# One head of each of four row groups per attention step, instead of two heads of each of two

## The chip, the core and the metric

The kernel runs on one core of a Trainium2 chip. The time is the device time of one launch in microseconds (us). Three runs of the kernel before gave 972.80, 970.39 and 972.62 us, median 972.62. All data is float32.

## The reference, cut to what matters

The reference is a two-layer transformer block on x of 4 sequences x 256 tokens x 512 features. Each layer is an attention and a feed-forward product, each followed by a residual sum and a layer norm. The change is in the attention of layer 0:

```python
q = (x @ Wq + bq).reshape(B, S, 32, 16)      # 32 query heads of 16
k = (x @ Wk + bk).reshape(B, S, 8, 16)       # 8 key heads, each serves 4 query heads
v = (x @ Wv + bv).reshape(B, S, 8, 16)
scores = q @ k.T / sqrt(16)                  # causal: a query sees the keys up to itself
p = softmax(where(causal, scores, -1e9))
out = (p @ v).reshape(B, S, 512) @ Wo + bo
```

Layer 1 has heads of 128 features and an ALiBi-like bias; the change doesn't touch it.

## The kernel before, in words

The program is written in a tile framework that draws the semaphores between the engines from what each instruction reads and writes, and that orders each engine's instructions when the program is built: it walks through the program with durations of its own, and lets an instruction that has to wait be passed by later ones. Each engine then runs its queue strictly in that order.

**Layer 0's attention.** `project0(b)` makes, for each of the four sequences b, `qT` and `kT` with the features on the partitions, and `v`. Partitions are read in four **row groups** of 32 rows. A row group r holds two key heads of 16 rows each, e = 0 and e = 1. `kT[:, e, :]` is the key tile with the rows of the other head set to zero, so that a product over the 32 rows of a group with `kT[rows, e]` gives the scores of head (r, e) alone. `qT[rows, i, :]` holds the i-th of the four query heads that share each key head.

A **step** is (b, qt, h, i): sequence, query tile of 128 queries (qt = 0 sees w = 128 keys, qt = 1 sees w = 256), pair of row groups h, query head i. There are 4 x 2 x 2 x 4 = 64 steps, and each works on four heads: row groups 2h and 2h+1, e = 0 and 1.

- `begin0` (lines 473 to 495): two score matmuls (L482), one for each row group, each 2w columns wide (both e), each into a PSUM bank of its own. So a step's tile `sc` takes two banks, and the pool `ps_s0` (L127) has two such tiles: four banks. Then VectorE adds the causal mask to the diagonal block (L487) and takes the negated row maxima (L490), and ScalarE makes four exponentials with row sums (L274, one for each head, each with an accumulator read after it). VectorE inverts the row sums (L279) and GpSimd multiplies the probabilities with them (L282), for the step before, through `divide0`.
- `transpose0` (L506 to L518), three steps later: TensorE transposes the four heads' probabilities, 128 x 128 at a time (L297), into a bank of the pool `ps_w`, and VectorE or ScalarE in turn (L100, L102) copies the bank to `prT`.
- `end0` (L520 to L541), after the fourth i of an h, with two steps more of delay: the value matmuls (L531). Each has 128 keys on the rows, 32 columns of `v` (one row group r, head e, the other head's 16 columns zero), and 512 moving columns (four i x 128 queries), and writes partitions 32r to 32r+31 of the bank `o`. The 32 columns are one **column group** of the array. Before the change the order is kt, e, then the two column groups of h. After h = 1 the bank is copied out and `tail0` (output product L438, layer norm, feed-forward product L455, layer norm) is queued.

Each float32 matmul of the program shows up in the trace as two matmul instructions, with two weight loads.

`run` (L323) issues the steps in the order begin, fill, transpose, end; `fill` advances the tails of the query tiles before (L438, L440, L455, L459, layer norms) and the projections of the sequence to come (L386, L399, L414). PSUM has 8 banks, all taken: 3 `ps_w`, 4 `ps_s0`, 1 `ps_o0`.

```python
    ps_s0 = pool(la, "ps_s0", 2, space=PSUM)
        sc = ps_s0.tile([P, 2, 2, 2 * P], F32, tag="s", name=f"sc_{name}")
        for j in range(2):
            rows = slice(32 * (2 * h + j), 32 * (2 * h + j) + 32)
```

Of the kernel before, what the change touches and what calls it, by code (L numbers as in the profile page):

```python
# [12 lines left out]
F32 = mybir.dt.float32  # L13
# [3 lines left out]
ALU = mybir.AluOpType  # L17
AX = mybir.AxisListType
PSUM = bass.MemoryType.PSUM

P = 128
B, S, D = 4, 256, 512
NTT = B * S // P
NC = D // P
NKV, G = 8, 4
BLK = 32
ROWS = 64
EPS = 1e-5
MASKED = -3.0e38

# [19 lines left out]
def distance_table():  # L52

    rel = P + np.arange(P)[:, None] - np.arange(2 * P)[None, :]
    dist = -np.sqrt(np.maximum(rel, 0).astype(np.float32))
    return np.where(rel >= 0, dist, np.float32(MASKED)).astype(np.float32)


@with_exitstack
def block_kernel(  # L60
# [20 lines left out]
    nc = tc.nc  # L81
    slopes = [float(s) for s in alibi_slopes()]

    def pool(stack, name, bufs=1, **kw):
        return stack.enter_context(tc.tile_pool(name=name, bufs=bufs, **kw))
# [9 lines left out]
    def evacuate(dst, src):  # L95

        if not last:
            turn[0] ^= 1
        if turn[0] and not last:
            nc.vector.tensor_copy(dst, src)  # L100
        else:
            nc.scalar.copy(dst, src)  # L102
# [18 lines left out]
    la = ctx.enter_context(ExitStack())  # L121
    wa = pool(la, "wa", side="right")
    a0 = pool(la, "a0", 2, side="right")
    causal = wa.tile([P, P], F32, name="causal")
    make_causal_mask(nc, causal, MASKED)
    ps_w = pool(ctx, "ps_w", 3, space=PSUM)
    ps_s0 = pool(la, "ps_s0", 2, space=PSUM)  # L127
    ps_o0 = pool(la, "ps_o0", 1, space=PSUM)
    ring = [ps_w, "w"]

# [102 lines left out]
    def load_weights1(kv):  # L233
        wq1 = w1.tile([P, NC, G * P], F32, tag="wq1", name=f"wq1_{kv}", bufs=1)
        wo1 = w1.tile([P, G, D], F32, tag="wo1", name=f"wo1_{kv}")
        if kv % 2 == 0:
            wk1 = w1.tile([P, NC, 2 * P], F32, tag="wk1", name=f"wk1_{kv}", bufs=1)
            nc.sync.dma_start(wk1, w_qkv_v[:, :, NQ + kv * P : NQ + (kv + 2) * P])
            wk_pair[kv // 2] = wk1
        nc.sync.dma_start(wq1, w_qkv_v[:, :, ts(kv, G * P)])  # L240
        weights1[kv] = (wq1, wo1)
        if kv == 0:
            load_output_weight(kv)
# [29 lines left out]
    def exponentials(pr, sc, nm, sums, i, w):  # L273
        nc.scalar.activation(  # L274
            pr[:, i, 0:w], sc, AF.Exp, bias=nm[:, i : i + 1], accum_out=sums[:, i : i + 1]
        )
# [9 lines left out]
    def softmax_tiles(sp, name, bufs):  # L286
        nm = sp.tile([P, G], F32, tag="nm", name=f"nm_{name}", bufs=bufs + 2)
        sums = sp.tile([P, G], F32, tag="sums", name=f"sums_{name}", bufs=bufs + 2)
        pr = sp.tile([P, G, 2 * P], F32, tag="pr", name=f"pr_{name}", bufs=bufs)
        return nm, sums, pr  # L290

    def transposed_probabilities(name, pr, parts):

        for kt, dst in parts:
            pt = bank_t(f"pt_{name}_{kt}")
            for i in range(G):
                nc.tensor.transpose(pt[:, i, :], pr[:, i, ts(kt, P)], ident)  # L297
            evacuate(dst, pt.rearrange("p i (j q) -> p i j q", q=32))
# [43 lines left out]
    def advance(queue):  # L342

        while queue:
            if next(queue[0], None) is not None:
                return
            queue.popleft()

    def exhaust(queue):
        while queue:  # L350
            advance(queue)
# [82 lines left out]
    def tail0(tt, oT):  # L434

        py = bank_m(f"py_{tt}")
        for i in range(G):
            nc.tensor.matmul(py, oT[:, i, :], wop[:, i, :], start=(i == 0), stop=(i == G - 1))  # L438
        y = s0.tile([P, D], F32, tag="y", name=f"y_{tt}")
        nc.vector.tensor_tensor(y, py, x[tt], ALU.add)  # L440
        factors = norm_factors(y, f"a{tt}")
        yield True
        x1 = s0.tile([P, D], F32, tag="x1", name=f"x1_{tt}")
        normalise(x1, y, factors)
        yield True
        if tt < NTT - 1:
            yield True
            yield True
        x1T = s0.tile([P, NC, P], F32, tag="x1T", name=f"x1T_{tt}")
        transposed(x1T, x1, f"x1_{tt}")  # L450
        nc.gpsimd.tensor_tensor(x1, x1, fb_b, ALU.add)
        yield True
        pf = bank_m(f"pf_{tt}")
        for c in range(NC):
            nc.tensor.matmul(  # L455
                pf, x1T[:, c, :], wfT[:, c, :], start=(c == 0), stop=(c == NC - 1)
            )
        y2 = s0.tile([P, D], F32, tag="y", name=f"y2_{tt}")
        nc.vector.tensor_tensor(y2, pf, x1, ALU.add)  # L459
        factors = norm_factors(y2, f"b{tt}")  # L460
        yield True
        x2[tt] = xp.tile([P, D], F32, tag="x", name=f"x2_{tt}")
        normalise(x2[tt], y2, factors)
        yield True
        if tt < NTT - 1:
            yield True
            yield True
        transposed(x2T[:, :, ts(tt, P)], x2[tt], f"x2_{tt}")
        yield True

    ahead, tails = deque(), deque()

    def begin0(b, qt, h, i):

        qT, kT, _ = qkv0[b]
        w = (qt + 1) * P
        name = f"0_{b}_{qt}_{h}_{i}"
        nm, sums, pr = softmax_tiles(a0, name, 6)
        sc = ps_s0.tile([P, 2, 2, 2 * P], F32, tag="s", name=f"sc_{name}")
        for j in range(2):  # L480
            rows = slice(32 * (2 * h + j), 32 * (2 * h + j) + 32)
            nc.tensor.matmul(  # L482
                sc[:, j, :, 0:w], qT[rows, i, ts(qt, P)], kT[rows, :, 0:w], start=True, stop=True
            )
        scf = sc.rearrange("p j e k -> p (j e) k")
        diag = scf[:, :, w - P : w]
        nc.vector.tensor_tensor(  # L487
            diag, diag, causal.unsqueeze(1).to_broadcast([P, G, P]), ALU.add
        )
        nc.vector.tensor_reduce(nm, scf[:, :, 0:w], AX.X, ALU.max, negate=True)  # L490
        for n in range(G):
            exponentials(pr, scf[:, n, 0:w], nm, sums, n, w)
        divide0()
        undivided.append((pr, sums, w))
        return pr

    open0 = {}
    undivided = []

    def divide0():  # L500


        if undivided:
            divided(*undivided.pop(), True)

    def transpose0(b, qt, h, i, pr):  # L506
        name = f"0_{b}_{qt}_{h}_{i}"
        if i == 0:
            open0["p", h] = a0.tile(
                [P, 2, G, 4, 4, 32], F32, tag="prT", name=f"prT0_{b}_{qt}_{h}"  # L510
            )
        prT = open0["p", h]
        transposed_probabilities(
            name,
            pr,
            [(kt, prT[:, kt, i].rearrange("p j n q -> p n j q")) for kt in range(qt + 1)],
        )
        return prT  # L518

    def end0(b, qt, h, i, prT):  # L520
        if i < G - 1:
            return
        if h == 0:
            open0["o"] = ps_o0.tile([P, G * P], F32, tag="o", name=f"o0_{b}_{qt}")
        o = open0["o"]
        v = qkv0[b][2]
        for kt in range(qt + 1):
            for e in range(2):
                for j in range(2):
                    r = 2 * h + j  # L530
                    nc.tensor.matmul(  # L531
                        o[32 * r : 32 * r + 32, :],
                        v[:, kt, r, ts(e, 32)],
                        prT[:, kt, :, :, 2 * j + e, :],
                        start=(kt == 0 and e == 0),
                        stop=(kt == qt and e == 1),
                    )
        if h == 1:
            oT = a0.tile([P, G, P], F32, tag="oT", name=f"oT0_{b}_{qt}")
            evacuate(oT.rearrange("p i q -> p (i q)"), o)  # L540
            tails.append(tail0(2 * b + qt, oT))  # L541

    def before0(step):
        b, qt, h, i = step
        if (qt, h, i) == (0, 0, 0):
            if b == 0:
                for _ in range(3):
                    advance(ahead)
            else:
                exhaust(ahead)  # L550
            if b + 1 < B:
                ahead.append(project0(b + 1))
            if b == 1:
                load_weights1(0)

    def fill():
# [3 lines left out]
    ahead.append(project0(0))  # L560
    tails.append(feed_forward_weight())
    run(
        [(b, qt, h, i) for b in range(B) for qt in range(2) for h in range(2) for i in range(G)],
        begin0,
        transpose0,
        end0,
        before0,
        fill,
        lag=3,
# [533 lines left out]
```

## Time and profile before

| what | value |
|---|---|
| median of three runs | 972.62 us (970.39 to 972.80) |
| the profiled execution's own time | 970.91 us |
| its span, first to last instruction | 968.9 us |
| mean granted TensorE clock | 0.995 |
| first to last score matmul of layer 0 (L482) | 14.1 to 253.7 us |
| first product of layer 1 (L632) | about 280 us |
| TensorE matmul busy, whole span | 97% |
| VectorE, ScalarE, GpSimd busy, whole span | 64%, 33%, 46% |

How to read it: times are us from the first instruction, single durations in ns. PE is TensorE's matmul, PEld its weight load, DVE VectorE, ACT ScalarE, POOL GpSimd. A "form" such as 32*128 32x512 is rows*columns of the array and the moving operand. The ends of matmuls are modelled, so that distances between starts are the better price of a matmul. Views of the trace used here: busy time by stretch, groups of instructions by line and form, the timeline, the chain of work, and waits.

### The profile page before, as it was taken

To read this page: it belongs to the slowest core of one execution; us is meant where nothing else is said; L and a number is where in the kernel's file an instruction comes from. 1 tells how busy PE (TensorE), PEld (TensorE's weight loads), DVE (VectorE), ACT (ScalarE), POOL (GpSimd) and SP (SyncE) were. 2 spreads that over 40 slices of the span, in tenths; PEclk is the share of its full clock that TensorE was granted. 3 is DMA by queue.
4 is the path that set the end of the run, shared out by engine and by line. 5 is a ranking of instruction groups with operands and counts; after the bars stand their busy time and mean duration, and the time that the engine had idled before them with its cause. 6 is when DMAs were issued, how large, how long until landed. Compare 5 with 4: busy or idle time off the path is not lost.

```text
span 968.9 us, 11389 instructions
## 1 busy us (share of the span) xinstructions
PE 939.5 (97%) x3593; PEld 556.0 (57%) x3593; DVE 619.7 (64%) x1291; ACT 316.3 (33%) x1194; POOL 445.6 (46%) x461
## 2 busy tenths in 40 slices
PE   7999999999899999999999999999999999999996
PEld 5645555554344445566666666666666666666652
DVE  3876767777633446665666665766676666666566
ACT  2664564555511002333222222122222212224441
POOL 3463552644446213444533553444633634556732
PEclk9999999999999999999999999999999999999998
DMA  9500000000020011354443443433443334332001
GB/s 237 185 1 1 1 1 1 1 1 1 1 87 0 22 44 39 103 139 120 122 134 90 123 133 109 130 109 87 131 130 91 128 77 119 113 105 69 1 33 55
DMA packets 76418, 74.45 MB, mean 77 GB/s; under 512 B 5957, under 2 KB 52678, under 8 KB 76358
## 3 DMA queue, kind: packets, MB, share of 16 engines
q1 hardware_dynamic: 75014, 72.02, 26.1%
q10 hardware_dynamic: 1344, 1.70, 0.6%
q8 instruction: 29, 0.48, 0.2%
q14 instruction: 31, 0.25, 0.1%
HBM read 49.58 MB, written 24.12 MB: 76 GB/s over the span
## 4 chain that ended last, share of the span: by engine, by line
PE 82%; POOL 9%; DVE 5%; ACT 2%; DMA 1%; issue 1%; ACTq 0%; POOLq 0%; DVEq 0%
PE p_q L632 18%; PE po L881 14%; PE sc L968 7%; PE o L1008 7%; PE p_k L632 5%; PE p_v L632 5%; PE o L531 5%; PE sc L482 4%; PE pt L297 3%; PE pq L399 3%; PE py L438 3%; PE pf L455 3%; PE py L842 2%; POOL pr L282 2%; POOL x L903 2%; ACT pr L274 1%
## 5 line engine op out<-in xcount | busy, mean ns | idle before, releaser
L274 ACT ACTIVATE pr<-sc,nm 128x256 f32<-128x256 f32 (+1 forms) x512 | 209.4, 420 | 364.7 <-DVE nm L984 277.2
L282 POOL TENSOR_TENSOR pr<-pr,sums 128x512 f32<-128x512 f32 (+1 forms) x128 | 190.1, 1485 | 232.1 <-DVE sums L279 223.9
L976 DVE SCALAR_TENSOR_TENSOR sc<-table,sc 128x128 f32<-128x128 f32 (+1 forms) x256 | 86.0, 356 | 34.7 <-PE sc L968 32.4
L274 ACT ACTIVATION_READ_ACCUMULATOR pr<-sc,nm 128x1 f32 x512 | 103.5, 202 | 0.0
L968 PEld LDWEIGHTS sc<-kT,qT 128*128 128x128 f32 x512 | 82.3, 191 | 35.1 <-issue 29.7
L968 PE MATMUL sc<-kT,qT 128*128 128x256 f32 (+1 forms) x512 | 95.0, 327 | 0.0
L1008 PE MATMUL o<-prT,v 128*128 128x512 f32 x192 | 92.8, 592 | 0.0
L308 DVE STREAM_TRANSPOSE blocks<-pr 128x512 f32<-128x512 f32 x84 | 57.6, 698 | 45.2 <-POOL pr L282 45.2
L646 DVE TENSOR_TENSOR qT<-p_q,qT 128x512 f32<-128x512 f32 x96 | 64.6, 685 | 33.6 <-PE p_q L632 32.8
L984 DVE TENSOR_REDUCE nm<-sc 128x2 f32<-128x512 f32 (+1 forms) x128 | 69.9, 550 | 1.5
L297 PE MATMUL pt<-ident,pr 128*128 128x128 f32 x432 | 62.6, 278 | 6.0 <-POOL pr L282 5.3
L297 PEld LDWEIGHTS pt<-ident,pr 128*128 128x128 f32 x432 | 49.3, 142 | 32.5 <-issue 17.1
L490 DVE TENSOR_REDUCE nm<-sc 128x4 f32<-128x512 f32 (+1 forms) x64 | 61.0, 953 | 1.1
L482 PE MATMUL sc<-kT,qT 32*128 32x256 f32 (+1 forms) x256 | 59.9, 533 | 1.6 <-ACT pr L274 1.6
L487 DVE TENSOR_TENSOR sc<-sc,causal 128x512 f32<-128x512 f32 x64 | 44.3, 692 | 26.5 <-PE sc L482 26.2
L881 PE MATMUL po<-wo,so 128*128 128x256 f32 x224 | 58.0, 381 | 2.1 <-POOL so L612 2.1
L632 PE MATMUL p_q<-x2T,ws_q 128*128 128x512 f32 x128 | 59.8, 592 | 0.0
L102 ACT COPY o<-o 128x512 f32<-128x512 f32 x29 | 17.0, 586 | 124.9 <-PE o L1008 124.9
L632 PE MATMUL p_q<-xt,ws_q 128*128 128x512 f32 x128 | 57.7, 592 | 0.0
L881 PE MATMUL po<-wo,o 128*128 128x256 f32 x224 | 57.7, 380 | 0.0
L632 PE MATMUL p_q<-x2T,wq 128*128 128x512 f32 x128 | 57.6, 592 | 0.0
L881 PE MATMUL po<-to,so 128*128 128x256 f32 x224 | 53.3, 381 | 1.0 <-POOL so L615 1.0
(155 smaller groups left out, 1435.2 us busy)
## 6 DMA issues: line engine op xcount, KB each, us to landing
way<-blocks SPq DMA_DIRECT2D x112, 128.0 KB, 2.5
prT<-way SPq DMA_DIRECT2D x28, 512.0 KB, 3.7
wq<-in_L_attn_w_qkv_dram SPq DMA_DIRECT2D x8, 1024.0 KB, 5.3
wo<-in_L_attn_w_o_dram SPq DMA_DIRECT2D x8, 1024.0 KB, 5.4
way<-blocks SPq DMA_DIRECT2D x112, 64.0 KB, 1.8
prT<-way SPq DMA_DIRECT2D x28, 256.0 KB, 2.6
wk<-in_L_attn_w_qkv_dram SPq DMA_DIRECT2D x4, 512.0 KB, 3.7
wv<-in_L_attn_w_qkv_dram SPq DMA_DIRECT2D x2, 1024.0 KB, 6.3
```

What stands on the lines that cost most here:

```text
L274: nc.scalar.activation(pr[:, i, 0:w], sc, AF.Exp, bias=nm[:, i : i + 1], accum_out=sums[:, i : i + 1])
L282: nc.gpsimd.tensor_tensor(pr[:, :, 0:w], pr[:, :, 0:w], sums.unsqueeze(2).to_broadcast([P, G, w]), ALU.mult)
L297: nc.tensor.transpose(pt[:, i, :], pr[:, i, ts(kt, P)], ident)
L482: nc.tensor.matmul(sc[:, j, :, 0:w], qT[rows, i, ts(qt, P)], kT[rows, :, 0:w], start=True, stop=True)
L490: nc.vector.tensor_reduce(nm, scf[:, :, 0:w], AX.X, ALU.max, negate=True)
L632: nc.tensor.matmul(bank, fixed, moving, start=(c == 0), stop=(c == 1))
L646: add = lambda dst, a, b: nc.vector.tensor_tensor(dst, a, b, ALU.add)
L881: nc.tensor.matmul(bank[:, ts(n, HALF)], left[:, c, :], right[:, c, :], start=(c == 0), stop=(c == 1),)
L968: nc.tensor.matmul(sc[:, m, 0:w], qT[:, 2 * j + m, b * S + qt * P : b * S + (qt + 1) * P], kT[:, b * S : b * S + w], start=True, stop=True,)
L976: nc.vector.scalar_tensor_tensor(sc[:, m, 0:w], table[:, 2 * P - w :], slopes[kv * G + 2 * j + m], sc[:, m, 0:w], ALU.mult, ALU.add,)
L984: nc.vector.tensor_reduce(nm[:, 2 * j : 2 * j + 2], sc[:, :, 0:w], AX.X, ALU.max, negate=True)
L1008: nc.tensor.matmul(o, v1[:, 2 * b + kt, ts(kv, P)], prT[:, kt].rearrange("p j h q -> p h j q"), start=(kt == 0), stop=(kt == qt),)
```

## The change

A step becomes (b, qt, e, i): one of the two heads e of each of **four** row groups. Its four score matmuls have w columns each (before: two with 2w), one in each of the four score banks. The pool of two tiles becomes one tile of four banks for the whole of layer 0, `scores0[P, 4, 2, 256]`, made once; the index in the third place, 0 or 1, is half a bank and alternates from step to step (`half0`). Mask, maxima, exponentials, transposes and copies keep their number and shapes; their third index now counts row groups. The value matmuls of an e go over the four column groups in turn; the accumulation of all four opens at e = 0 and closes at e = 1, four steps later. The number of value matmuls is the same.

```diff
-    ps_s0 = pool(la, "ps_s0", 2, space=PSUM)
+    ps_s0 = pool(la, "ps_s0", 1, space=PSUM)
...
+    scores0 = ps_s0.tile([P, 4, 2, 2 * P], F32, name="scores0")
+    half0 = [0]
+
+    def begin0(b, qt, e, i):
...
-        sc = ps_s0.tile([P, 2, 2, 2 * P], F32, tag="s", name=f"sc_{name}")
-        for j in range(2):
-            rows = slice(32 * (2 * h + j), 32 * (2 * h + j) + 32)
+        half0[0] ^= 1
+        sc = scores0[:, :, half0[0], :]
+        for r in range(4):
+            rows = slice(32 * r, 32 * r + 32)
             nc.tensor.matmul(
-                sc[:, j, :, 0:w], qT[rows, i, ts(qt, P)], kT[rows, :, 0:w], start=True, stop=True
-            )
-        scf = sc.rearrange("p j e k -> p (j e) k")
-        diag = scf[:, :, w - P : w]
+                sc[:, r, 0:w], qT[rows, i, ts(qt, P)], kT[rows, e, 0:w], start=True, stop=True
+            )
+        diag = sc[:, :, w - P : w]
...
-            exponentials(pr, scf[:, n, 0:w], nm, sums, n, w)
+            exponentials(pr, sc[:, n, 0:w], nm, sums, n, w)
...
-    def end0(b, qt, h, i, prT):
+    def end0(b, qt, e, i, prT):
...
         for kt in range(qt + 1):
-            for e in range(2):
-                for j in range(2):
-                    r = 2 * h + j
-                    nc.tensor.matmul(
-                        o[32 * r : 32 * r + 32, :],
-                        v[:, kt, r, ts(e, 32)],
-                        prT[:, kt, :, :, 2 * j + e, :],
-                        start=(kt == 0 and e == 0),
-                        stop=(kt == qt and e == 1),
-                    )
-        if h == 1:
+            for r in range(4):
+                nc.tensor.matmul(
+                    o[32 * r : 32 * r + 32, :],
+                    v[:, kt, r, ts(e, 32)],
+                    prT[:, kt, :, :, r, :],
+                    start=(kt == 0 and e == 0),
+                    stop=(kt == qt and e == 1),
+                )
+        if e == 1:
```

In the list of steps, and in `transpose0` and `before0`, h is renamed e.

More of the change, by code (lines that the diff above doesn't have):

```diff
@@ L471, in block_kernel @@
     ahead, tails = deque(), deque()
-    def begin0(b, qt, h, i):
+    scores0 = ps_s0.tile([P, 4, 2, 2 * P], F32, name="scores0")
+    half0 = [0]
+    def begin0(b, qt, e, i):
         qT, kT, _ = qkv0[b]
         w = (qt + 1) * P
-        name = f"0_{b}_{qt}_{h}_{i}"
+        name = f"0_{b}_{qt}_{e}_{i}"
         nm, sums, pr = softmax_tiles(a0, name, 6)
-        sc = ps_s0.tile([P, 2, 2, 2 * P], F32, tag="s", name=f"sc_{name}")
-        for j in range(2):
-            rows = slice(32 * (2 * h + j), 32 * (2 * h + j) + 32)
+        half0[0] ^= 1
+        sc = scores0[:, :, half0[0], :]
+        for r in range(4):
+            rows = slice(32 * r, 32 * r + 32)
             nc.tensor.matmul(
-                sc[:, j, :, 0:w], qT[rows, i, ts(qt, P)], kT[rows, :, 0:w], start=True, stop=True
+                sc[:, r, 0:w], qT[rows, i, ts(qt, P)], kT[rows, e, 0:w], start=True, stop=True
             )
-        scf = sc.rearrange("p j e k -> p (j e) k")
-        diag = scf[:, :, w - P : w]
+        diag = sc[:, :, w - P : w]
         nc.vector.tensor_tensor(
@@ L489, in begin0 @@
         )
-        nc.vector.tensor_reduce(nm, scf[:, :, 0:w], AX.X, ALU.max, negate=True)
+        nc.vector.tensor_reduce(nm, sc[:, :, 0:w], AX.X, ALU.max, negate=True)
         for n in range(G):
-            exponentials(pr, scf[:, n, 0:w], nm, sums, n, w)
+            exponentials(pr, sc[:, n, 0:w], nm, sums, n, w)
         divide0()
@@ L504, in divide0, with transpose0 @@
             divided(*undivided.pop(), True)
-    def transpose0(b, qt, h, i, pr):
-        name = f"0_{b}_{qt}_{h}_{i}"
+    def transpose0(b, qt, e, i, pr):
+        name = f"0_{b}_{qt}_{e}_{i}"
         if i == 0:
-            open0["p", h] = a0.tile(
-                [P, 2, G, 4, 4, 32], F32, tag="prT", name=f"prT0_{b}_{qt}_{h}"
+            open0["p", e] = a0.tile(
+                [P, 2, G, 4, 4, 32], F32, tag="prT", name=f"prT0_{b}_{qt}_{e}"
             )
-        prT = open0["p", h]
+        prT = open0["p", e]
         transposed_probabilities(
@@ L518, in transpose0 @@
         return prT
-    def end0(b, qt, h, i, prT):
+    def end0(b, qt, e, i, prT):
         if i < G - 1:
             return
-        if h == 0:
+        if e == 0:
             open0["o"] = ps_o0.tile([P, G * P], F32, tag="o", name=f"o0_{b}_{qt}")
@@ L543, in before0 @@
     def before0(step):
-        b, qt, h, i = step
-        if (qt, h, i) == (0, 0, 0):
+        b, qt, e, i = step
+        if (qt, e, i) == (0, 0, 0):
             if b == 0:
@@ L562, in block_kernel @@
     run(
-        [(b, qt, h, i) for b in range(B) for qt in range(2) for h in range(2) for i in range(G)],
+        [(b, qt, e, i) for b in range(B) for qt in range(2) for e in range(2) for i in range(G)],
         begin0,
```

## The prediction

> **What bounds the kernel now.** I read first the page's busy shares and slices, to find layer 0's attention and its busiest engine.
>
> ```profile
> PE 939.5 (97%) x3593; PEld 556.0 (57%) x3593; DVE 619.7 (64%) x1291; ACT 316.3 (33%) x1194; POOL 445.6 (46%) x461
> ...
> PE   7999999999899999999999999999999999999996
> ```
>
> A slice is 24.2 us; by the lines in the trace the attention fills slices 1 to 11. PE is nearly always busy, but a busy PE may be only waiting between modelled ends. So second, busy time by stretch, with the stretch cut at the first and last score matmuls (L482):
>
> ```profile
> 14.10:253.60 239.50, 234.86 (x1163) 127.60 (x1162) 178.36 (x340) 137.62 (x555) 115.91 (x90) 1.00 0.10 27
> 253.60:290.00 36.40, 32.44 (x119) 14.31 (x119) 14.55 (x28) 8.87 (x26) 15.93 (x13) 0.95 0.17 58
> ```
>
> The columns are length, then PE, PEld, DVE, ACT, POOL busy. PE has 234.9 of 239.5 us; DVE is second with 178.4. Third, PE's waits in that region: the only ones of L482 are
>
> ```profile
> PE sc L482 <- ACT pr L274: 1.6, 4, 0.4
> ```
>
> (total us, times, longest). Scores almost never wait for a free score tile: two tiles are enough. Adding up start-to-start distances of PE's matmuls gives 57.6 us for scores, 38.3 for values, 48.7 for transposes; the rest are projections and tails. **PE's queue bounds the stage**; 63 step periods take 239.5 us, 3.8 us each.
>
> Fourth, what one step is made of, by form:
>
> ```profile
> L274 ACT ACTIVATE pr<-sc,nm 128x128 f32<-128x128 f32 x123 | 43.6, 367 | 28.9 <-DVE sums L279 26.4 <-PE sc L482 1.7 <-DVE nm L490 0.6
> L487 DVE TENSOR_TENSOR sc<-sc,causal 128x512 f32<-128x512 f32 x62 | 42.9, 692 | 24.3 <-PE sc L482 24.0
> ...
> L490 DVE TENSOR_REDUCE nm<-sc 128x4 f32<-128x1024 f32 x32 | 39.1, 1220 | 0.7
> ...
> L490 DVE TENSOR_REDUCE nm<-sc 128x4 f32<-128x512 f32 x30 | 20.5, 685 | 0.4
> ```
>
> and the timeline of one step of qt = 1, with the next step's scores:
>
> ```profile
> 99.82 1.13 PE L482 MATMUL sc<-kT,qT 32*128 32x512 f32 x4
> ...
> 101.00 0.70 DVE L487 TENSOR_TENSOR sc<-sc,causal 128x512 f32<-128x512 f32 x1 [0.38 <-PE sc L482]
> ...
> 101.73 1.22 DVE L490 TENSOR_REDUCE nm<-sc 128x4 f32<-128x1024 f32 x1
> ...
> 103.31 1.13 PE L482 MATMUL sc<-kT,qT 32*128 32x512 f32 x4
> ...
> 104.77 0.21 ACT L274 ACTIVATION_READ_ACCUMULATOR pr<-sc,nm 128x1 f32 x1
> ```
>
> The exponentials (474 ns each at 256 columns) start at 103.05. The reader is to see that the next scores start at 103.31, while ScalarE still reads this step's scores until 104.98. From score to last read such a step takes 5.16 us, more than the 3.8 us period: the stage lives on **two score sets in flight**.
>
> **What the Trainium skill says.** (1) "PSUM — Partial Sum Buffer", section "PSUM bank collisions raise a hardware error": two engines must not be in the same bank on the same 32 partitions together, even at disjoint columns, and software has to order them. All accesses here span all partitions. So halves of a bank can't be two buffers: step n+1's score matmul into bank r must wait for step n's exponential of bank r. The trace shows such an order: in layer 1 two score products fill the halves of one bank, and VectorE's first instruction on the first half waits for both:
>
> ```profile
> 452.78 1.89 PE L968 MATMUL sc<-kT,qT 128*128 128x256 f32 x8
> ...
> 453.84 1.29 DVE L976 SCALAR_TENSOR_TENSOR sc<-table,sc 128x256 f32<-128x256 f32 x3 [0.17 <-PE sc L968]
> ```
>
> By single records the first half's product ends at 453.38, the second's at 453.81; VectorE starts at 453.84. (2) "TensorEngine Tiling (Array Packing)", "Gotcha 1: PSUM Pressure": row tiles that run together need different banks; four row groups therefore take all four score banks. (3) "TensorE: Matmul & The Clock Gate", "Measured speedup vs the span model": four row tiles of 32 rows and 512 columns ran 3.07 times as fast as one by one. No run here shows four yet; two do run as one, since two row groups' records start 7 ns apart.
>
> **The change, part by part.**
>
> *Scores, PE.* 256 matmul instructions become 512 of half the width, and weight loads as many. By single records the second pass of a set starts 0.53 us after the first at 512 columns, 0.32 at 256; a set takes 1.13 and 0.70 us. If four row groups run as two do, qt = 1 takes 0.70, and qt = 0 (128 columns: second pass at 0.22, plus 0.27) about 0.50, an estimate. Saved: 32 x 0.43 + 32 x 0.20 = 20 us of PE. The doubled loads (0.18 us each) go to different row groups side by side. Bounds: none of the packing beyond two gives 0 saved and 0.2 to 0.3 us more per set.
>
> *Values, PE.* In the same stretch of the timeline 8 instructions of two column groups take 1.91 us: four pairs 0.44 apart, plus the last one's 0.59. Four groups halve the 38.3 us: 19 saved; bounds 0 and 19. PE's need falls from 239.5 to about 200 us.
>
> *The wait.* Now the chain from step to step is serial: scores, mask, maxima, four exponentials with the last accumulator read, next scores. The mask reads all four banks, so releasing them one by one gains nothing: the last bank's matmul alone takes as long as the set. With gaps from the timeline (0.05, 0.03, 0.10, and 0.05 from read to matmul, as in the four waits above):
> - qt = 1: 0.70 + 0.05 + 0.70 + 0.03 + 1.22 + 0.10 + 1.95 + 0.05 = 4.8 us
> - qt = 0: 0.50 + 0.05 + 0.69 + 0.03 + 0.69 + 0.10 + 1.51 + 0.05 = 3.6 us
>
> 32 x 3.6 + 31 x 4.8 = **264 us** as a floor, against 239.5.
>
> *Other work in the chain's way.* In the trace before, adding up what VectorE and ScalarE ran in the gaps between scores, mask, maxima and exponentials, without other steps' maxima, gives 40 us (copies L100 and L102 27, layer norms 11): 0.63 us a step. VectorE's masks and maxima are 64 x (0.69 + 0.95) = 105 us; its other 178.4 - 105 = 73 us filled 55% of the time that the chain left it; over about 300 us it fills 37%. So 0.63 x 0.37 / 0.55 = 0.42 us a step, 27 us. Bounds: 0.1 and 0.9.
>
> *Uneven PE work.* Queued behind a waiting score matmul are transposes, values, projections and tails. They have room on average (200 of 300 us), but some periods hold up to 6.9 us of PE work, and older work goes first. Taking each old period less its saving, and the larger of that and the chain, adds 9 us (5 to 13).
>
> Sum: 264 + 27 + 9 = 300 us, **+60**. After the last score the PE backlog is gone: the last step's multiplied probabilities, ready at 264.3, were transposed only from 270.4, and the last values' 3.6 us halve: -5 (-9 to 0). Layer 1 doesn't change. Nothing goes to the DMA queues; GpSimd's 116 us has room. The accumulator bank `o` is held as long as before.
>
> 970.9 + 60 - 5 = **1026 us**. The profiled execution, 970.9, lies within the runs shown, 1.7 below their median; I leave that.
>
> **Rivals.**
> 1. *The halves work as two buffers* (scores written beside the exponentials' reads). Then PE stays the bound with 39 us less: 932 us, or up to 950 with VectorE (178 us) and the chain in the way. For it: PE's full row. Against it: (1) and L976's start. It decides if a score set starts before the exponentials of the step before have ended. 7%; with 2% for a gain and loss that cancel.
> 2. *The chain at its bare price*: other work fits into the holes. 264 + 0 to 13, less 5 to 9: 986 to 1000 us. For it: PE idles a third of the time, so copies come early. Against it: 0.63 us a step today. 9%.
> 3. *Four row groups don't run as four*: sets of 0.95 and 0.70 us, 63 x 0.22 = +14 us: about 1040 us, up to 1075 with the high contention. The doubled weight loads speak for it, the 7 ns starts against it. 10%.
>
> **How the numbers follow.** My own case, 72%: 1026 us, from 264 + 6 + 13 - 239.5 - 9 = +35 (contention 0.1) up to 264 + 57 + 6 - 239.5 = +88: 1005 to 1059. The range 1000 to 1060 leaves out rival 1, most of 2 and the top of 3. Slower 0.91, faster 0.07, within 0.3% (what a measurement of this kernel can tell from no change) 0.02.
>
> **What would show it.** In the changed profile: waits of PE sc L482 for ACT pr L274 at the top of PE's list, some 60 times; each score set starting about 0.05 us after an accumulator read; sets of 0.70 and 0.50 us; sixteen values in about 2 us instead of 3.6; PE at about two thirds in the stage, DVE and ACT less dense; the first L632 near 335 us instead of 280, and the time after it unchanged. Wrong if score sets start while the step before is still being read, or if periods average under 4.1 us.

## The result, and the profile after

The changed kernel takes 1104.38 us (median of four runs, 1104.16 to 1105.58) against 971.5 us before (four runs): a ratio of 1.137, 95% interval 1.1349 to 1.1391. Each ratio below is against runs of the kernel before that were made beside it (medians 971.5 to 971.8 us). It is slower, as forecast, but by 133 us where 55 were forecast and 88 were the far end.

The page's busy shares and slices of the changed kernel (PE's row and the granted clock in tenths):

```profile
PE 956.4 (87%) x3849; PEld 578.3 (52%) x3849; DVE 625.1 (57%) x1291; ACT 319.5 (29%) x1194; POOL 443.9 (40%) x461
...
PE   7756856777575669999999999999999999999996
...
PEclk9777978778786779999999999999999999999998
```

A slice is now 27.6 us. For 15 slices PE is half to eight tenths busy, where it was at nine before, and its clock falls to about 0.8. Busy time by stretch, cut at the first and last score matmuls and about at the start of layer 1 (columns as in the prediction; the clock follows POOL's):

```profile
14.28:394.94 380.66, 258.39 (x1445) 151.33 (x1445) 187.33 (x346) 143.94 (x565) 116.15 (x91) 0.79 0.06 17
394.94:431.30 36.36, 31.64 (x106) 15.52 (x106) 13.22 (x25) 6.04 (x15) 17.36 (x14) 0.87 0.17 59
```

The stage grew from 239.5 to 380.7 us, +141. The way from the last score set to layer 1's first product fell from 26.5 (253.55 to 280.03) to 19.9 us (394.94 to 414.81), -6.6. From there to the end it is 688.9 and 688.8 us: all of the difference is in layer 0's attention.

The waits of PE in that stretch, in place of the few us of before:

```profile
PE pt L299 <- POOL pr L284: 113.0, 40, 5.2
PE scores L488 <- ACT pr L276: 3.2, 1, 3.2
```

Scores (now L488) wait for ScalarE's reads almost never, and transposes (now L299) wait for GpSimd's product 40 times. That isn't the picture that the prediction drew. A score set is the score matmuls of one step. Two sets of the last sequence on PE's timeline show how it comes about:

```profile
373.19 0.71 PE L488 MATMUL scores<-kT,qT 32*128 32x256 f32 x8
...
379.59 1.97 PE L299 MATMUL pt<-ident,pr 128*128 128x128 f32 x8 [4.77 <-POOL pr L284]
381.49 0.81 PE L488 MATMUL scores<-kT,qT 32*128 32x256 f32 x4
```

These are the scores of steps 60 and 61. The last read of step 60's scores ended at 379.42, so the scores of step 61 could have started at 379.47. But eight transposes of step **59** stand ahead of them in PE's queue. They had waited until 379.54 for GpSimd's product of step 59, and took 1.97 us at a low clock. Why was that product so late? The same stretch on the other engines:

```profile
376.18 1.22 DVE L495 TENSOR_REDUCE nm<-scores 128x4 f32<-128x1024 f32 x1
377.31 0.17 DVE L281 RECIPROCAL sums<-sums 128x4 f32<-128x4 f32 x1
...
377.65 1.89 POOL L284 TENSOR_TENSOR pr<-pr,sums 128x1024 f32<-128x1024 f32 x1 [1.97 <-DVE sums L281]
```

The reciprocal of step 59 is pinned behind the maxima of step 60 (`divide0`), and the product takes 1.89 us after it. So a second chain leads from one score set to the next, beside the one through the exponentials: scores n, mask, maxima n, reciprocal n-1, product n-1, transposes n-1, scores n+1. Before the change the transposes between scores n and n+1 were those of step n-3, with products long done. Single records show the move: before, 348 of the 384 transposes ran three score sets after their own; now 309 run one set after it. We read it as the work of the builder of the order, which sees PE free while the scores wait and moves transposes two steps forward. They are then in the queue ahead of the scores, and the scores, though free to start at 379.47, start only behind them.

Adding up single records of all steps gives the bill of the stage (us; "other work" is the time between the chain's links beyond the bare gaps):

| part of the chain, 64 steps | predicted | after |
|---|---|---|
| score sets | 38 | 50.9 |
| mask, maxima, exponentials | 216 | 215.8 |
| bare gaps between them | 11.5 | 11.5 |
| other work between them | 27 | 29 |
| last read to next scores | 12 | 78.6 |
| sum, less the last step's chain of 5 | 300 | 380.7 |

In the 78.6 us PE ran transposes for 50, projections, tails and values for 24, and was idle for 4. So the 113 us of waiting for GpSimd run mostly beside the chain through the exponentials. What is paid for is that the transposes are held until about the time when the scores could start, and then run in front of them.

### The profile page after: what moved, and what is told of

It is laid out like the page before. It is cut to its first block, busy times and chain, and to the rows that moved or that the text cites. A ratio compares the mean times of both kernels' runs of the same rounds, so it can differ in the third digit from the quotient of the medians.

```text
span 1103.6 us, 11993 instructions
## 1 busy us (share of the span) xinstructions
PE 956.4 (87%) x3849; PEld 578.3 (52%) x3849; DVE 625.1 (57%) x1291; ACT 319.5 (29%) x1194; POOL 443.9 (40%) x461
## 4 chain that ended last, share of the span: by engine, by line
PE 69%; POOL 14%; DVE 12%; issue 3%; ACT 1%; DMA 1%; POOLq 0%; DVEq 0%; ACTq 0%
PE p_q L635 16%; PE po L884 12%; POOL pr L284 7%; PE sc L971 6%; PE o L1011 6%; PE pt L299 5%; PE p_k L635 4%; PE p_v L635 4%; DVE nm L495 4%; PE scores L488 3%; PE pf L457 3%; PE py L440 3%; DVE scores L492 3%; PE py L845 2%; POOL x L906 1%
## 5 line engine op out<-in xcount | busy, mean ns | idle before, releaser
L276 ACT ACTIVATE pr<-sc,nm 128x128 f32<-128x128 f32 (+1 forms) x256 | 105.0, 419 | 291.1 <-DVE nm L987 277.2
L299 PE MATMUL pt<-ident,pr 128*128 128x128 f32 x432 | 81.6, 334 | 119.2 <-POOL pr L284 118.3
L276 ACT ACTIVATE pr<-scores,nm 128x128 f32<-128x128 f32 (+1 forms) x256 | 104.3, 420 | 166.7 <-DVE sums L281 159.5
L299 PEld LDWEIGHTS pt<-ident,pr 128*128 128x128 f32 x432 | 60.7, 170 | 157.4 <-POOL pr L284 148.0
L102 DVE COPY prT<-pt 128x512 f32<-128x512 f32 x43 | 29.5, 687 | 87.9 <-PE pt L299 87.9
L492 DVE TENSOR_TENSOR scores<-scores,causal 128x512 f32<-128x512 f32 x64 | 44.5, 696 | 57.7 <-PE scores L488 51.8
L495 DVE TENSOR_REDUCE nm<-scores 128x4 f32<-128x512 f32 (+1 forms) x64 | 61.1, 955 | 1.7
L104 ACT COPY prT<-pt 128x512 f32<-128x512 f32 x65 | 37.7, 588 | 69.8 <-PE pt L299 69.8
```

What stands on the lines that cost most here:

```text
L276: nc.scalar.activation(pr[:, i, 0:w], sc, AF.Exp, bias=nm[:, i : i + 1], accum_out=sums[:, i : i + 1])
L492: nc.vector.tensor_tensor(diag, diag, causal.unsqueeze(1).to_broadcast([P, G, P]), ALU.add)
L495: nc.vector.tensor_reduce(nm, sc[:, :, 0:w], AX.X, ALU.max, negate=True)
```

## The experiments

**1. Is it the single score set, or the packing?** The kernel before, with one score tile:

```diff
-    ps_s0 = pool(la, "ps_s0", 2, space=PSUM)
+    ps_s0 = pool(la, "ps_s0", 1, space=PSUM)
```

> The kernel before, with one score tile (two banks) in place of two; packing, steps and values as before. Theory: what costs is that only one score set is in flight, not the packing. Then it is about as slow as the changed kernel, or slower by what its wider score sets (1.13 and 0.70 us in place of 0.71 and 0.50) and two-group values add to the chain: 1105 to 1160 us. Rival: the packing itself (tile modes, doubled weight loads, a lower granted clock) costs the 133 us: then this one stays within 965 to 1000 us.

Measured: 1140.29 us, ratio 1.1726 (1.1707 to 1.1746). Taking the second set away costs 169 us by itself, with two row groups and two column groups as before. PE's waits show the same picture as the changed kernel:

```profile
PE pt L297 <- POOL pr L282: 91.0, 33, 4.4
PE sc L482 <- ACT pr L274: 3.2, 1, 3.2
```

Last read to next scores is 87.6 us, score sets take 75.3. The move of the transposes comes with the single set too (289 of 384 run one set after their own), and so does the low clock, 0.79 in the stage. The packing isn't the loss: beside this kernel the changed one is 36 us faster, 24 of them in the score sets.

**2. Do the two halves of a bank buy anything?**

```diff
-        half0[0] ^= 1
+        half0[0] = 0
```

> The changed kernel, with every step in the same half of the score banks (the half index is always 0). Theory: a bank is what is waited for, so that the second half buys nothing: 1101 to 1108 us. Rival: the halves let a part of the scores overlap the reads of the step before: slower by more than 5 us.

Measured: 1103.31 us (1102.54 to 1104.18), against 1104.38 for the changed kernel. The alternating half is worth nothing. Why, this run can't say: in both kernels the scores stand behind other work of PE, and wait for ScalarE's reads just once (3.2 and 3.1 us). Experiment 3 says more.

**3. The order on PE.** The transposes of step n-3 are queued behind the scores of step n, an edge that sets the order only:

```diff
-            nc.tensor.matmul(
+            issued[:] = [nc.tensor.matmul(
                 sc[:, r, 0:w], qT[rows, i, ts(qt, P)], kT[rows, e, 0:w], start=True, stop=True
-            )
+            )]
...
-        transposed_probabilities(
+        with tc.issue_after(issued[0].ins):
+          transposed_probabilities(
```

> The changed kernel, with the transposes of step n-3 queued behind the scores of step n on TensorE, as the order stood before; nothing else changes. Theory A: TensorE's queue has the transposes of step n-1 ahead of the scores of step n+1, and they wait for GpSimd's product; this makes most of the 78.6 us between the last accumulator read and the next score set, which falls to about 10: 1030 to 1055 us. Rival B: the chain through mask, maxima and exponentials with a throttled clock is what costs, and the wait before the transposes only fills idle time: 1090 to 1106 us.

Measured: 1063.18 us, ratio 1.0951 (1.091 to 1.0992). That is 41 us back, 8 us short of the window of theory A and far from rival B. PE's longest waits have changed places:

```profile
PE scores L489 <- ACT pr L276: 80.5, 37, 4.2
PE o L536 <- DVE prT L102: 9.5, 7, 2.3
```

This is the picture that the prediction drew. Of the 63 sets after the first, 38 start 0.05 us after the last read of the step before, and none starts ahead of it, although the halves alternate:

```profile
54.17 0.19 ACT L276 ACTIVATION_READ_ACCUMULATOR pr<-scores,nm 128x1 f32 x1
...
55.52 0.21 ACT L276 ACTIVATION_READ_ACCUMULATOR pr<-scores,nm 128x1 f32 x1
...
55.79 0.71 PE L489 MATMUL scores<-kT,qT 32*128 32x256 f32 x8 [1.85 <-ACT pr L276]
```

The first head's scores had been read by 54.4, and yet all four row groups wait for the fourth read: the program hands the four banks over as one. It uses neither halves nor single banks as buffers. The order between the engines is drawn by the framework and the same in every run, so what the chip would do without it is not shown.

The time from last read to next scores fell from 78.6 to 33.0 us, not to 10: what PE still has in front of the scores is mostly tails (L457 and L440, 20 us). Other work in the chain rose from 29 to 43 us, most of it between mask and maxima (from 9.7 to 16.1 us, bare gap included), where copies of earlier transposes take 10.3 us of VectorE instead of 3.6, and before the exponentials (from 7.3 to 12.5). The clock in the stage is 0.82 (0.79 in the changed kernel). The profiled execution took 1070.9 us, the longest of the four, so these figures of the stage are some 8 us long in sum.

**4. An earlier product.** Each step's reciprocal and product follow its own exponentials:

```diff
-        divide0()
-        undivided.append((pr, sums, w))
+        divided(pr, sums, w)
```

> The changed kernel, with each step's reciprocal and product issued right after its own exponentials, not behind the next step's maxima. Theory A: transposes of step n-1 stay ahead of scores n+1 in TensorE's queue, but their probabilities are now ready some 3 us sooner, before the exponentials of step n have ended, so the queue hardly waits: 1030 to 1060 us. Rival B, as for the run with another order: 1090 to 1106 us. A third possibility: the reciprocal, waiting for the exponentials, blocks copies behind it on VectorE: slower than 1106 us.

Measured: 1116.15 us, ratio 1.1474 (1.1453 to 1.1495), slower than the changed kernel by 12 us. Theory A failed here; the time is where the third possibility put it. Transposes of step n-1 still run before scores n+1, and PE's idle time before them fell from 119 to 53 us; last read to next scores fell to 46.2. But now ScalarE's queue has the copy of those transposes ahead of the exponentials. Its waits are headed by

```profile
ACT prT L104 <- PE pt L299: 150.2, 48, 6.1
```

where the changed kernel has 55.8 us in 47. Between maxima and exponentials 40.3 us went by, instead of 7.3, and between mask and maxima 31.3 instead of 9.7. What the third possibility named is there too: VectorE's reciprocals wait for the exponentials for 66.6 us, 49 times, a wait that the changed kernel doesn't have. No run takes the two apart. The waits before the transposes shrank on PE, and waits at the heads of the other two queues grew.

**5. Both edits together.** The diffs of experiments 3 and 4.

> The changed kernel with both edits: transposes of step n-3 queued behind the scores of step n, and each step's reciprocal and product right after its own exponentials. Theory: with transposes three steps back nothing waits for the product any more, so the early product gives nothing beyond the order alone: 1055 to 1070 us. Rival: the two add up, because copies behind late transposes stand before masks and exponentials: 1030 to 1050 us.

Measured: 1061.97 us, ratio 1.0942 (1.0917 to 1.0967), within 1.3 us of the order alone. With transposes three steps back an earlier product has nothing left to give; the two don't add up. Its profiled execution (1062.8 us) has a stage of 340.3 us: score sets 46.3, other work 42, last read to next scores 29.2.

**6. The clock.** On top of experiment 3, two products a step that nothing reads, right behind the scores:

```diff
+WARM = 2
...
+        if WARM:
+            with tc.issue_after(issued[0].ins):
+                warm = bank_m(f"warm_{name}")
+                for m in range(WARM):
+                    nc.tensor.matmul(warm, ident, wq[:, m].rearrange("p i n -> p (i n)"), start=True, stop=True)
```

> The changed kernel with its transposes behind the scores, and two extra 128x512 products a step right behind the scores, whose result nothing reads (about 1.75 us of TensorE a step at full clock). Theory: TensorE's idle gaps lower its granted clock (about 0.8 in the stage), and that lengthens the score sets and the projections and tails in front of the next scores; with the gaps filled the clock stands near 1.0, the score sets take 0.71 and 0.50 us throughout, and in spite of 111 us of added work the time stays within 1045 to 1070 us. Rival: the clock doesn't follow the idleness: the sets stay as long as they are, and the added work shows up in full where it delays scores: above 1085 us.

Measured: 1064.84 us, ratio 1.0967 (1.095 to 1.0984), against 1063.18 without them. Busy time in the stage, by the same cut:

```profile
14.10:352.80 338.70, 314.91 (x1668) 173.93 (x1668) 191.26 (x345) 138.16 (x563) 115.44 (x91) 0.99 0.07 20
```

The clock stands at 0.99, where it was 0.82. Nearly all transposes run three sets after their own in both runs, so it is the filling of the gaps that raised the clock. All but 3 of the 64 score sets took 0.50 or 0.71 us, where 29 of the changed kernel's were longer, up to 1.24. Some 111 us of added work (128 products of about 0.87 us, an estimate from two matmul instructions 0.44 apart) cost next to nothing in sum. Score sets fell from 47.4 to 41.5 us and other work from 43 to 23, while last read to next scores rose from 33.0 to 52.1. What the clock gives back and what the added work takes can't be told apart by this run.

**7. The same filling in the changed kernel as it is**, without the rule on the transposes.

> The changed kernel as it is, with two extra 128x512 products a step behind the scores, whose result nothing reads, and no rule on the transposes. The order that the builder makes of it has the transposes of step n-3 or n-2 between two score sets again, since TensorE now looks taken while the scores wait. Theory: order and clock are both mended by the filling, so 111 us of added work make the changed kernel faster, close to the run with both edits: 1058 to 1075 us. Rival: added work on the engine in front of the chain only adds: above 1104 us.

Measured: 1064.37 us, ratio 1.0951 (1.0917 to 1.0985): 40 us **faster** than the changed kernel, with 111 us more work on PE. PE's waits for GpSimd are gone from the list:

```profile
PE scores L488 <- ACT pr L276: 21.1, 19, 2.8
PE scores L488 <- DVE qT L404: 2.6, 4, 0.7
```

In the trace 352 of the 384 transposes run three sets after their own, as in experiment 6, and the stage is as long (338.5 and 338.8 us). This is what the expectation foresaw of a builder to which PE no longer looks free. Beside experiment 3, which reaches 1063.18 us by the order alone, the added products bring nothing more: the 40 us are about what the order is worth, and the full clock pays for the added work.

**8. The part of the change that needs no score bank.** The kernel before, with the values of both h issued together over four column groups; for the room, three `prT`, five `pr` and one `oT` buffer:

```diff
+        done0[h] = prT
+        if h == 0:
+            return
...
             for e in range(2):
-                for j in range(2):
-                    r = 2 * h + j
+                for r in range(4):
                     nc.tensor.matmul(
...
-                        prT[:, kt, :, :, 2 * j + e, :],
+                        done0[r // 2][:, kt, :, :, 2 * (r % 2) + e, :],
```

> The kernel before (two row groups, two score tiles), with the values of both h issued together after h = 1 and over four column groups in turn; for the room, three prT buffers instead of two, five pr buffers instead of six, one oT buffer instead of two. Theory: TensorE's queue bounds the stage, so the 19 us that four column groups save show up, less some waiting at the larger burst of values: 953 to 964 us. Rival: another engine is close enough behind (VectorE 178 of 239.5 us, the chains of the steps) that little comes through: 967 to 973 us. Slower, above 975 us, if the fewer buffers hold the steps back.

Measured: 956.46 us (956.14 to 961.05), ratio **0.9858** (0.9836 to 0.9881): faster than both kernels. The timeline shows 30 of a query tile's 32 value instructions in 3.63 us, which is what 16 took before. Before:

```profile
68.12 3.63 PE L531 MATMUL o<-prT,v 128*32 128x512 f32 x16
```

Here:

```profile
144.29 3.63 PE L533 MATMUL o<-prT,v 128*32 128x512 f32 x30
```

and the stage, cut at its first and last score matmuls, has PE as full as before at a full clock:

```profile
13.90:241.50 227.60, 222.72 (x1163) 124.11 (x1162) 177.23 (x340) 136.81 (x555) 115.63 (x90) 1.00 0.09 29
```

By distances between starts the 160 value instructions in the stage took 25.0 us, against 38.3; the stage is 11.9 us shorter (239.5 to 227.6), and the way from the last score set to layer 1's first product 2.0 us (26.5 to 24.5).

**9. A control for the buffers.** Experiment 8's buffer counts alone.

> The kernel before with only the buffer counts of the values-only run (three prT, five pr, one oT): a control. Theory: the gain of the values-only run is from the four column groups: 969 to 975 us here. Rival: the third prT buffer brings it: 955 to 963 us.

Measured: 972.33 us, ratio 1.0 (0.9986 to 1.0014). The buffer counts are not the gain of experiment 8; it is from the order of the values.

## Why the prediction was right or wrong

**Right: what bounded the kernel.** PE's queue did: four column groups for the values alone shorten the stage (experiment 8), with 13 us of the 19 foreseen in the stage itself.

**Right: halves are no buffers, and one set is in flight.** Experiment 3 shows that sets wait for the last read of the step before, whichever half they write; what is waited for is the tile of four banks as a whole. Experiment 1 shows that the lost second set is the whole reason for the sign. The rule that the prediction took from the Trainium skill's page "PSUM — Partial Sum Buffer", section "PSUM bank collisions raise a hardware error", is tested by no run here, as the program keeps it in all of them.

**Right: four row groups run as one.** The timeline shows sets of eight matmuls in 0.71 us at 256 columns, and single records 0.50 at 128, as worked out, where the clock is full; sixteen values over four column groups took 1.92 us. No run has the row groups one after the other, so the factor 3.07 that the prediction cites isn't tested. Rival 3 is out, and so are rival 1 and, by far, rival 2. (By its own terms rival 2 reaches up to 264 + 13 - 239.5 - 5 = +33, 1003 us, not 1000; nothing rests on it.)

**Right: the chain's instructions,** 216 us, and the end, -5, measured -6.6.

**Right by luck: other work in the chain, 27 us;** measured 29. The estimate assumed the old order and a stage of 300 us. With the order put back (experiment 3) the same term is 43 us, and with the gaps of PE filled besides (experiment 6) it is 23.

**Wrong: "Uneven PE work", 9 us.** This step failed. It took from the order of before how much PE work stands ahead of the scores, and said that transposes queued *behind* a waiting score matmul have room. The order was built anew. Transposes of step n-1 came to stand *ahead* of the scores, held there by GpSimd's product, and the interval from last read to next scores measured 78.6 us where 12 were reckoned (3 for the bare gap, 9 for this). Putting the order back gives 41 of the 78 us missing (experiments 3 and 5), and the prediction's expected wait appears only then.

**Wrong: score sets at a full clock.** They measured 50.9 us instead of 38; 29 of 64 took up to 1.24 us. The prediction had PE idle for a third of the stage and still used prices of a full PE. The Trainium skill's page "TensorE: Matmul & The Clock Gate", section "HAM oscillation — how this bites in real kernels", warns of this: idle gaps bring the clock down, and the work after them starts slow. It belonged in the prediction. The trace agrees: 0.79 with gaps, 0.99 with the gaps filled. The page names gaps of more than about 3.4 us. In the changed kernel's stage 11 of PE's 48 gaps (idle for more than 0.15 us) are longer than that; but in experiment 4 only 2 of 83 are, and the clock is 0.80 all the same, so here shorter gaps go with a low clock too. The low clock also lengthened the transposes and tails ahead of the scores (eight transposes 1.97 us, against 1.04 at a full clock). Of the 66 us too few in the interval, 46 go with the order alone (experiment 3, at a clock of 0.82); how much of the other 21 is clock stays open.

**Too small even with the order put back.** Experiment 3's stage is 345.9 us, not 300 (experiment 5's is 340.3): sets 47.4, other work 43, interval 33.0. The rest is spread over the low clock, tails ahead of scores, and copies in the chain; no run takes these apart.

## What to carry to other kernels

Count the sets in flight before the width of the array: packing that doubles the banks of a set takes away the second set, and the step's whole chain becomes its period; here one set in flight cost 169 us without the packing, of which the packing gave 36 back. Where an order is built from expected durations, a new wait can change the order around it: here transposes were moved into the hole, and as they waited for a slower engine, they held up the scores behind them; look at which step's work lies between two waiting instructions. Take the half of a change that needs no scarce buffer by itself: the values alone give 1.4%.

## What the runs showed that was not expected

Adding 111 us of useless products to the engine at the end of the chain made the changed kernel 40 us faster (1104.38 to 1064.37). The order that came with them is worth about as much alone (1063.18), and the full clock paid for their time. And making a product ready sooner made the kernel 12 us slower (1116.15), with longer waits at the heads of two other engines' queues.
